# Extremes of a pair of chunks by a difference on GpSimd and fused passes on VectorE, in the FFN of an attention block

## The chip, the core and the metric

The kernel runs on one core of a Trainium2 chip. The metric is device time in microseconds (us). A core has five engines with queues of their own: TensorE (PE; PEld is its weight load), VectorE (DVE), ScalarE (ACT), GpSimd (POOL) and SyncE (SP, which only issues transfers here). An engine works through its own instructions in order; between engines, semaphores carry the order.

## What is computed

A cross-attention with a residual, and then a feed-forward network (FFN) whose two layers multiply quantized numbers, for 32 batches of 100 rows of 256:

```python
def _affine_quantize(x):
    amin, amax = (jnp.min(x), jnp.max(x))
    scale = jnp.maximum((amax - amin) / 255.0, 1e-08)
    zp = jnp.clip(jnp.round(-amin / scale) + QMIN, QMIN, QMAX)
    q = jnp.clip(jnp.round(x / scale) + zp, QMIN, QMAX)
    return (q, scale, zp)
...
    h = _qlinear(x, W1, b1)
    h = jax.nn.gelu(h, approximate=False)
    out = _qlinear(h, W2, b2)
...
x = x + _L0_xattn_ref(_layernorm(x, axis=-1), ctx_1024, ctx_1024, ...)
x = x + _L0_ffn_ref(_layernorm(x, axis=-1), L0_ffn_W1, L0_ffn_b1, L0_ffn_W2, L0_ffn_b2)
```

What matters here is `amin` and `amax` of `h`, the whole tensor after the gelu: 1024 features for 3200 rows. Nothing of the second layer can be quantized before both are known.

## The kernel before

The attention takes most of the kernel. Its last part, the residual of the last batch, ends near 1246 us of the profile; then comes the FFN.

**First layer.** `h` lies in SBUF as 128 partitions x 8 chunks of features (`fc`) x 3200 rows, in fp32. The rows are taken in five units `u`: two of 400 rows (g 0 and 1) and three of 800 (two groups of 400 each). For every unit and every chunk TensorE makes a product in PSUM (L823), and ScalarE applies the gelu on the way to `h` (L831). Below, (u, fc) names one such chunk. Between these, ScalarE rounds the input rows of later groups (`round_rows`, L738), GpSimd clips them (`bound_rows`, L752, writing `xq`), TensorE turns them (L777) and ScalarE copies them back (`turn`, L780).

**Extremes.** As soon as a span of chunks is done, VectorE takes its maximum (L838, a column of `hmax`) and its minimum (L840, a column of `hmin`), each a pass of its own over all elements of the span. `spans` says how many chunks go together: two in units 2 and 3 (1600 elements a partition), four in unit 4 (3200). `follow` and the variable `after` write out the order of VectorE's work by hand. In the end L861 and L862 reduce the columns to `ext2`, the maximum and the negated minimum of each partition.

**Parameters.** `affine_params` lets GpSimd reduce `ext2` over the partitions (`partition_all_reduce`, L108, result `alh`), and VectorE works out scale, reciprocal and bounds in a chain of tiny instructions (L110 to L126). Ahead of it, GpSimd runs an all-reduce on a dummy `g2` (L855 to L857), after its last `xq`.

**Second layer.** For ten blocks of rows ScalarE and VectorE scale `h` to integers (`ih`, L895 and L891), VectorE clips them (`hq`, L900), TensorE multiplies (`pf`, L908), VectorE adds the residual (L876), and SyncE stores. The first block is one of 128 rows. In front of it TensorE runs 18 products on an idle tile (`warm`, L151 to L156), released by a tiny product that reads the last column of `hmax`.

The tiles of the first layer lie in a pool `f1`, which is closed before the second layer's pool `f2` opens.

Of the kernel before, what the change touches and what calls it, by code (L numbers as in the profile page):

```python
# [8 lines left out]
F32 = mybir.dt.float32  # L9
BF16 = mybir.dt.bfloat16  # L10
I16 = mybir.dt.int16
AF = mybir.ActivationFunctionType
ALU = mybir.AluOpType
AX = mybir.AxisListType
# [7 lines left out]
BIG = 3.4e38  # L22
# [5 lines left out]
def kernel(  # L28
# [15 lines left out]
    nc = tc.nc  # L44
    P = 128
    B, T, D = x.shape
# [11 lines left out]
    NG = B // G  # L58
    GT = G * T
# [7 lines left out]
    const = ctx.enter_context(tc.tile_pool(name="const", bufs=1))  # L67
# [27 lines left out]
    def follow(a, b):  # L95

        tc.add_manual_dep(a.ins, b.ins.name, ORDER)
# [53 lines left out]
    def warm(ps, n, gate=None):  # L151

        if gate is not None:
            nc.tensor.matmul(ps[: gate.shape[1], : gate.shape[1]], gate, gate, start=True, stop=True)
        for _ in range(n):
            nc.tensor.matmul(ps, idle[:, :P], idle, start=True, stop=True)  # L156


    with ExitStack() as att:
# [120 lines left out]
        def v_part(b, h, s):  # L280

            c = cbuf[b % NCB]
            if s == 0:
                vs[b, h] = p1.tile([SC, NSC, E // 2], F32, tag=f"v{h}", name=f"v{b}_{h}")
            pv = bank(f"pv{b}_{h}_{s}")
            for dc in range(NDC):
                nc.tensor.matmul(  # L287
                    pv[:SC, :],
                    c[:, dc, s * SC : (s + 1) * SC],
                    wvt[h][:, dc, :],  # L290
                    start=(dc == 0),
                    stop=(dc == NDC - 1),
                )
            return nc.vector.tensor_copy(vs[b, h][:, s, :], pv[:SC, :])  # L294
# [321 lines left out]
        for i, (b, first, n) in enumerate(steps):  # L616
            g, j = b // G, b % G
# [5 lines left out]
            if b >= 1:  # L623
                for h in begun:
                    for c in range(NSC):
                        done = v_part(b, h, c)
# [9 lines left out]
            for h in ended:  # L636
                k = 2 * j + h
# [26 lines left out]
        i = len(steps) - 1  # L664
# [17 lines left out]
    f1 = ff1.enter_context(tc.tile_pool(name="f1", bufs=2))  # L682
    ps_h = ctx.enter_context(tc.tile_pool(name="ps_h", bufs=3, space=PSUM))
# [4 lines left out]
    h = hpool.tile([P, NFC, N], F32, tag="h", name="h")  # L688
# [41 lines left out]
    ixs, xqs = {}, {}  # L730

    def round_rows(g, engine, after):
        ixs[g] = f1.tile([T, G * D], I16, tag="ix", name=f"ix{g}", bufs=3)
        src = xg[g].rearrange("t b d -> t (b d)")
        if engine is nc.vector:
            done = nc.vector.tensor_scalar(ixs[g], src, rx[:T], None, ALU.mult)
        else:
            done = nc.scalar.activation(ixs[g], src, AF.Copy, bias=0.0, scale=rx[:T])  # L738
        if after is not None:
            follow(done, after)  # L740
        return done

    def bring_back(g):

        if g < len(places):
            first, n = places[g]
            nc.sync.dma_start(out=xf[g][:, :n, :], in_=rows(xb2, first, n))

    def bound_rows(g, engine, after=None):
        xqs[g] = f1.tile([T, G * D], BF16, tag="xq", name=f"xq{g}", bufs=4)  # L750

        done = engine.tensor_scalar(  # L752
            xqs[g], ixs[g], hix[:T], QMIN - QMAX, ALU.min, ALU.max
        )
        if after is not None:
            follow(done, after)
        bring_back(g)
        return done
# [5 lines left out]
    units = [(0, 1), (1, 1)] + [(g, 2) for g in range(2, NG, 2)]  # L764
# [3 lines left out]
    def turn(g, part, parts):  # L768

        if part == 0:  # L770
            xqTs[g] = f1.tile([P, NDC, GT], BF16, tag="xqT", name=f"xqT{g}", bufs=4)
        n = G // parts
        pt = ps_t.tile([P, NDC, 512], BF16, tag="pt", name=f"pty{g}_{part}")
        for dc in range(NDC):
            for j in range(n):
                k = (part * n + j) * D + dc * P
                nc.tensor.transpose(  # L777
                    pt[:, dc, j * T : (j + 1) * T], xqs[g][:, k : k + P], identb[:T, :T]
                )
        done = nc.scalar.copy(  # L780
            xqTs[g][:, :, part * n * T : (part + 1) * n * T], pt[:, :, : n * T]
        )
        if gelu is not None:
            follow(done, gelu)

    NR = 20
    hmax = f1.tile([P, NR], F32, tag="hmax", name="hmax", bufs=1)
    hmin = f1.tile([P, NR], F32, tag="hmin", name="hmin", bufs=1)
    k = 0
# [4 lines left out]
    after = scaled  # L794
    for part in range(2):
        sl = slice(part * G * D // 2, (part + 1) * G * D // 2)
        nc.scalar.activation(i0[part], src[:, sl], AF.Copy, bias=0.0, scale=rx[:T])
        after, before = nc.vector.tensor_scalar(
            xq0[:, sl], i0[part], QMIN - QMAX, hix[:T], ALU.max, ALU.min
        ), after  # L800
# [3 lines left out]
    after = round_rows(1, nc.vector, after)  # L804
    after = bound_rows(1, nc.vector, after)
# [2 lines left out]
    turned = {(0, 4): 1, (1, 2): 2, (1, 6): 3, (2, 4): 4, (2, 6): 5, (3, 4): 6, (3, 6): 7}  # L808
    for u, (g, n) in enumerate(units):
        ts = slice(g * GT, (g + n) * GT)  # L810
        spans = ((1, 1, 2, 2, 2), (2, 2, 4), (2,) * 4, (2,) * 4, (4, 4))[u]
        ends = [sum(spans[: i + 1]) for i in range(len(spans))]
        for fc in range(NFC):
            if (u, fc) in turned:
                turn(turned[u, fc], 0, 1)

            cut = 2 if (u, fc) == (0, 0) else 1
            m = GT // cut
            for part in range(cut):
                ph = ps_h.tile([P, 2, 512], F32, tag="ph", name=f"ph{u}_{fc}_{part}")  # L820
                for i in range(n):
                    for dc in range(NDC):
                        nc.tensor.matmul(  # L823
                            ph[:, i, :m],
                            w1qt[:, dc, fc * P : (fc + 1) * P],
                            xqTs[g + i][:, dc, part * m : (part + 1) * m],
                            start=(dc == 0),
                            stop=(dc == NDC - 1),
                        )
                at = slice(g * GT + part * m, g * GT + part * m + n * m)  # L830
                gelu = nc.scalar.activation(  # L831
                    h[:, fc, at].rearrange("p (k t) -> p k t", k=n),
                    ph[:, :n, :m],
                    AF.Gelu, bias=b1t[:, fc : fc + 1], scale=c1,
                )
                if fc + 1 in ends:
                    src = h[:, fc + 1 - spans[ends.index(fc + 1)] : fc + 1, at if cut > 1 else ts]
                    done = nc.vector.tensor_reduce(hmax[:, k : k + 1], src, AX.XY, ALU.max)  # L838
                    follow(done, after)
                    after = nc.vector.tensor_reduce(hmin[:, k : k + 1], src, AX.XY, ALU.min)  # L840
                    k += 1
            if (u, fc) == (0, 1):
                after = round_rows(2, nc.vector, after)

                done = bound_rows(2, nc.gpsimd, reduced)
                added = keep(B - 1, nc.gpsimd, nc.gpsimd)
                follow(added, done)
                normalize(B - 1, added, nc.gpsimd)
            if (u, fc) in rounded:
                i = rounded[u, fc]  # L850
                round_rows(i, nc.scalar, gelu)
                bound_rows(i, nc.gpsimd)

    g2 = small.tile([P, 1], F32, tag="g2", name="g2")
    nc.gpsimd.tensor_copy(g2, epst)  # L855
    nc.gpsimd.tensor_copy(g2[:T], xqs[NG - 1][:, 0:1])
    nc.gpsimd.partition_all_reduce(g2, g2, P, bass_isa.ReduceOp.max)  # L857

    ext2 = const.tile([P, 2], F32, tag="ext2", name="ext2")
    with tc.high_priority():  # L860
        nc.vector.tensor_reduce(ext2[:, 0:1], hmax[:, :k], AX.X, ALU.max)  # L861
        nc.vector.tensor_reduce(ext2[:, 1:2], hmin[:, :k], AX.X, ALU.min, negate=True)  # L862
        rh, hih, c2, _, _, found, bounds, product = affine_params(ext2, "h", scales["2"][1])
    warm(ps_h.tile([P, 512], F32, tag="ph", name="warm3"), 18, hmax[:, k - 1 : k])

    ff1.close()
    f2 = ctx.enter_context(tc.tile_pool(name="f2", bufs=2))
# [1 line left out]
    after = found  # L869
# [12 lines left out]
    for i, (first, n) in enumerate(blocks):  # L882
        hq = f2.tile([P, NFC, G * P], BF16, tag="hq", name=f"hq{i}", bufs=3)
        ts = slice(first * P, (first + n) * P)
        ih = []
        for k in range(2):
# [3 lines left out]
            if k == 1 and i in halved:  # L890
                done = nc.vector.tensor_scalar(t, h[:, sl, ts], rh, None, ALU.mult)  # L891
                follow(done, after)
                after = done
            else:
                nc.scalar.activation(t, h[:, sl, ts], AF.Copy, bias=0.0, scale=rh)  # L895
        if i == 0:
            after = bounds(after)
        for k in range(2):
            sl = slice(k * NF2, (k + 1) * NF2)
            done = nc.vector.tensor_scalar(  # L900
                hq[:, sl, : n * P], ih[k], QMIN - QMAX, hih, ALU.max, ALU.min
            )
            follow(done, after)
            after = done
# [10 lines left out]
        if i == 0:  # L915
            after = product(after)
        if i >= 2:
            done = finish(i - 2)
            follow(done, after)
            after = done  # L920
# [43 lines left out]
```

## Time and profile before

| | us |
|---|---|
| median of three runs (1339.32 to 1339.75) | 1339.72 |
| the profiled execution | 1340.4 |
| its span | 1338.6 |
| TensorE busy in the span | 1306.3 (98%) |
| VectorE busy | 779.1 (58%) |
| ScalarE busy | 696.2 (52%) |
| GpSimd busy | 96.4 (7%) |
| first gelu begins, last gelu ends | 1251.5, 1293.3 |
| first product of the second layer begins | 1312.1 |

The span is what the hardware profiler recorded from first to last instruction of one execution; the execution is 1.8 us longer. The page cuts the span into 40 slices of 33.5 us and gives each engine's busy share of a slice in tenths; the last two slices hold the FFN:

```profile
PE   9999999999999999999999999999999999999748
DVE  4666446664366554664366653664566543576897
PEclk9999999999999999999999999999999999999989
```

PEclk is the clock that TensorE was granted, in tenths of its full speed. In the groups of instructions a row reads: line, engine, operation, what is written <- what is read, shapes, count, then busy us and mean ns of one, then idle time before it and whose event ended that. In a timeline a row begins with start and duration in us, and a row of several instructions is merged; durations overlap the next start by a little, so the time that an instruction takes of its engine is read from start to start.

### The profile page before, as it was taken

To read this page: it belongs to the slowest core of one execution; us is meant where nothing else is said; L and a number is where in the kernel's file an instruction comes from. 1 tells how busy PE (TensorE), PEld (TensorE's weight loads), DVE (VectorE), ACT (ScalarE), POOL (GpSimd) and SP (SyncE) were. 2 spreads that over 40 slices of the span, in tenths; PEclk is the share of its full clock that TensorE was granted. 3 is DMA by queue.
4 is the path that set the end of the run, shared out by engine and by line. 5 is a ranking of instruction groups with operands and counts; after the bars stand their busy time and mean duration, and the time that the engine had idled before them with its cause. 6 is when DMAs were issued, how large, how long until landed. Compare 5 with 4: busy or idle time off the path is not lost.

```text
span 1338.6 us, 25468 instructions
## 1 busy us (share of the span) xinstructions
PE 1306.3 (98%) x10062; PEld 807.5 (60%) x10064; DVE 779.1 (58%) x2391; ACT 696.2 (52%) x1927; POOL 96.4 (7%) x190
## 2 busy tenths in 40 slices
PE   9999999999999999999999999999999999999748
PEld 4666556666566566666566666665666665666426
DVE  4666446664366554664366653664566543576897
ACT  2555345565355455563355454553455543554865
POOL 1000000200011000110011000110001000110200
PEclk9999999999999999999999999999999999999989
DMA  8010001000000000000000000000000000000212
GB/s 254 20 44 13 12 12 44 19 18 1 12 19 18 12 12 1 19 19 12 12 18 19 12 2 12 18 18 12 12 13 18 18 2 12 11 10 5 61 41 99
DMA packets 24864, 33.02 MB, mean 25 GB/s; under 512 B 1828, under 2 KB 22792, under 8 KB 24744
## 3 DMA queue, kind: packets, MB, share of 16 engines
q1 hardware_dynamic: 21776, 24.81, 6.3%
q0 software_dynamic: 2144, 5.38, 1.3%
q8 instruction: 79, 1.29, 0.4%
q10 hardware_dynamic: 824, 1.19, 0.3%
q14 instruction: 41, 0.34, 0.1%
HBM read 24.82 MB, written 6.55 MB: 23 GB/s over the span
## 4 chain that ended last, share of the span: by engine, by line
PE 94%; issue 3%; ACT 2%; DVE 0%; POOL 0%; POOLq 0%; DVEq 0%
PE pv L287 25%; PE pk L256 23%; PE sc L423 13%; PE av L468 10%; PE pt L373 7%; PE pq L348 6%; PE py L505 6%; PE pf L908 2%; ACT h L831 1%; PE po L489 1%; PE po L519 0%; PE ptx L336 0%; ACT ix L738 0%; ACT xqT L780 0%; PE pk L270 0%
## 5 line engine op out<-in xcount | busy, mean ns | idle before, releaser
L287 PE MATMUL pv<-wvt,c 128*128 128x512 f32 x768 | 338.3, 596 | 0.0
L256 PE MATMUL pk<-c,wkt 128*128 128x361 f32 x1016 | 314.2, 467 | 0.0
L263 ACT COPY kT<-pk 128x361 f32<-128x361 f32 x254 | 117.0, 461 | 366.4 <-PE pk L256 366.4
L404 ACT ACTIVATE p<-p,m 114x361 f32<-114x361 f32 x512 | 297.3, 590 | 7.8 <-DVE m L434 7.8
L256 PEld LDWEIGHTS pk<-c,wkt 128*128 128x128 f32 x1016 | 191.9, 190 | 113.2 <-issue 1.0
L434 DVE CUSTOM_DVE_ANT_0 p<-sc,maskt 114x361 f32<-114x361 f32 x512 | 252.2, 533 | 11.9 <-PE sc L423 6.9
L287 PEld LDWEIGHTS pv<-wvt,c 128*128 128x128 f32 x768 | 143.3, 190 | 172.1 <-issue 161.7
L385 DVE COPY pT<-pt 128x300 f32<-128x300 f32 x50 | 22.3, 468 | 351.6 <-PE pt L373 351.6
L423 PE MATMUL sc<-kT,q 64*114 64x361 f32 x1024 | 208.4, 490 | 0.0
L385 ACT COPY pT<-pt 128x300 f32<-128x300 f32 x462 | 168.9, 414 | 73.8 <-PE pt L373 71.2
L373 PEld LDWEIGHTS pt<-ident,p 50*128 50x128 f32 x3072 | 131.1, 139 | 78.0 <-issue 51.5
L449 DVE TENSOR_SCALAR p<-p,r 114x361 f32<-114x361 f32 x512 | 173.5, 402 | 2.6
L294 DVE COPY v<-pv 128x512 f32<-128x512 f32 x192 | 129.3, 679 | 28.7 <-PE pv L287 28.3
L468 PEld LDWEIGHTS av<-pT,v 128*64 128x64 f32 x3072 | 132.8, 137 | 18.5 <-ACT pT L385 15.0
L468 PE MATMUL av<-pT,v 128*64 128x100 f32 x3072 | 140.0, 250 | 0.0
L373 PE MATMUL pt<-ident,p 50*128 50x50 f32 x3072 | 133.5, 221 | 0.3 <-DVE p L449 0.3
L404 ACT ACTIVATION_READ_ACCUMULATOR p<-p,m 114x1 f32 x512 | 99.1, 194 | 0.0
L135 POOL TENSOR_TENSOR xb<-x,b2a 100x256 f32<-100x256 f32 x32 | 23.5, 733 | 900.4 <-DVE rmax L529 891.2
L348 PE MATMUL pq<-xnT,wqt 128*128 128x400 f32 x256 | 87.9, 500 | 0.2 <-ACT xnT L339 0.2
L423 PEld LDWEIGHTS sc<-kT,q 64*114 64x114 f32 x1024 | 76.7, 184 | 4.3 <-issue 0.6
L505 PE MATMUL py<-aT,wot 128*128 128x400 f32 x224 | 76.4, 499 | 0.0
L443 DVE RECIPROCAL r<-rsum 114x4 f32<-114x4 f32 (+1 forms) x131 | 22.8, 174 | 90.2 <-ACT p L404 89.9
(125 smaller groups left out, 720.0 us busy)
## 6 DMA issues: line engine op xcount, KB each, us to landing
c<-in_ctxT_dram SPq DMA_DIRECT2D x31, 361.0 KB, 3.2
x<-in_x_dram SPq DMA_DIRECT2D x8, 400.0 KB
xb<-xb POOLq DMA_DIRECT2D x32, 100.0 KB, 2.1
x<-xb SPq DMA_DIRECT2D x5, 384.0 KB, 3.1
out_dram<-ot SPq DMA_DIRECT2D x3, 384.0 KB, 2.6
wqt<-in_wq_dram SPq DMA_DIRECT2D x4, 256.0 KB
wot<-in_wo_dram SPq DMA_DIRECT2D x1, 1024.0 KB, 8.5
w<-in_w1T_dram POOLq DMA_DIRECT2D x1, 1024.0 KB, 5.5
```

What stands on the lines that cost most here:

```text
L256: nc.tensor.matmul(pk[:, :S], wkt[q][:, dc, col * P : (col + 1) * P], c[:, dc, :S], start=(dc == 0), stop=(dc == NDC - 1),)
L287: nc.tensor.matmul(pv[:SC, :], c[:, dc, s * SC : (s + 1) * SC], wvt[h][:, dc, :], start=(dc == 0), stop=(dc == NDC - 1),)
L294: return nc.vector.tensor_copy(vs[b, h][:, s, :], pv[:SC, :])
L348: nc.tensor.matmul(pq[:, :GT], wqt[q][:, dc, pair * P : (pair + 1) * P], xnTs[g][:, dc, :], start=(dc == 0), stop=(dc == NDC - 1),)
L373: nc.tensor.transpose(pts[k][:SC, (h * NSC + c) * TH : (h * NSC + c + 1) * TH], pb[ks, h0 + h, c * SC : (c + 1) * SC], ident[ks, ks],)
L385: copies.append(copy(pT[:, :, k, :], src))
L404: done = nc.scalar.activation(s, s, AF.Exp, bias=ms[h], scale=-1.0, accum_out=rsum[:, h : h + 1])
L423: nc.tensor.matmul(pss[h][:TP, :S], qbuf[pair // PAIRS][k * DK : (k + 1) * DK, pair % PAIRS, j, :, :].rearrange("p k t -> p (k t)")[:, :TP ...
L434: found = nc.vector.tensor_tensor_reduce(pb[:, h, :S], pss[h][:TP, :S], maskt, 1.0, BIG, ALU.add, ALU.min, ms[h])
L449: nc.vector.tensor_scalar(s, s, r[:, h : h + 1], None, ALU.mult)
L468: nc.tensor.matmul(av[k * DK : (k + 1) * DK, (pair - p0) * T : (pair - p0 + 1) * T], vs[b, pair // HP][:, c, h * DK : (h + 1) * DK], pTs[i ...
L505: nc.tensor.matmul(py[:, :GT], wot[:, c, dc * P : (dc + 1) * P], aT[:, c, :, :].rearrange("p j t -> p (j t)"), start=(c == 0), stop=(c == ...
```

## The change

Four pairs of neighbouring chunks, (2,6) with (2,7), (3,6) with (3,7), (4,0) with (4,1) and (4,6) with (4,7), are taken out of the reductions. With a the first and b the second of a pair, GpSimd forms r = max(a - b, 0) in two instructions. Then max(a, b) = r + b, and -min(a, b) = r - a. VectorE runs one fused pass for each of the two: it adds or subtracts two tensors of 800 elements a partition, and takes the maximum of the results and of a starting column. The elementwise result goes to `other`, which nobody reads. Unit 4 is reduced in pairs now, and its chunks 2 to 5 still by two passes each.

The starting columns chain the passes: pair (2,6) begins from -BIG and runs in the middle of unit 3; after the last reduction, `hmax` and `hmin` are reduced, merged with its result, and handed through pairs (3,6), (4,0) and (4,6); the last writes `ext2`. The dummy all-reduce now follows the last difference, and the idle products wait for the first column of pair (4,0).

```diff
+    paired = {(2, 6): (3, 3), (3, 6): (3, 7), (4, 0): (4, 1), (4, 6): (4, 7)}
+    diffs = {}
+
+    def difference(u, fc):
+        g, n = units[u]
+        ts = slice(g * GT, (g + n) * GT)
+        a, b = h[:, fc, ts], h[:, fc + 1, ts]
+        r = f1.tile([P, 2 * GT], F32, tag="r", name=f"r{u}_{fc}", bufs=4)
+        nc.gpsimd.tensor_tensor(r, a, b, ALU.subtract)
+        nc.gpsimd.tensor_scalar(r, r, 0.0, None, ALU.max)
+        diffs[u, fc] = r, a, b
+
+    def pair(u, fc, ext, behind, after):
+
+        r, a, b = diffs[u, fc]
+        for col, (x, op) in enumerate(((b, ALU.add), (a, ALU.subtract))):
+            other = f1.tile([P, 2 * GT], BF16, tag="other", name=f"other{u}_{fc}_{col}", bufs=1)
+            done = nc.vector.tensor_tensor_reduce(
+                other, r, x, 1.0, ext[col], op, ALU.max, behind[:, col : col + 1]
+            )
+            follow(done, after)
+            after = done
+        return after
...
-        spans = ((1, 1, 2, 2, 2), (2, 2, 4), (2,) * 4, (2,) * 4, (4, 4))[u]
+        spans = ((1, 1, 2, 2, 2), (2, 2, 4))[u] if u < 2 else (2,) * 4
...
-                if fc + 1 in ends:
+                if fc + 1 in ends and (u, fc - 1) not in paired:
...
+            for p, at in paired.items():
+                if at == (u, fc):
+                    difference(*p)
+            if (u, fc) == (3, 3):
+                after = pair(2, 6, (-BIG, -BIG), exts[0], after)
...
-    nc.gpsimd.tensor_copy(g2[:T], xqs[NG - 1][:, 0:1])
+    nc.gpsimd.tensor_copy(g2, diffs[4, 6][0][:, 0:1])
...
+    done = nc.vector.tensor_reduce(exts[1][:, 0:1], hmax[:, :k], AX.X, ALU.max)
+    follow(done, after)
+    after = nc.vector.tensor_reduce(exts[1][:, 1:2], hmin[:, :k], AX.X, ALU.min, negate=True)
+    done = nc.vector.tensor_tensor(exts[1], exts[1], exts[0], ALU.max)
+    follow(done, after)
+    after = done
+    cols = [exts[1][:, 0:1], exts[1][:, 1:2]]
+    for p, behind in (((3, 6), exts[2]), ((4, 0), exts[3]), ((4, 6), ext2)):
+        after = pair(*p, cols, behind, after)
+        cols = [behind[:, 0:1], behind[:, 1:2]]
     with tc.high_priority():
-        nc.vector.tensor_reduce(ext2[:, 0:1], hmax[:, :k], AX.X, ALU.max)
-        nc.vector.tensor_reduce(ext2[:, 1:2], hmin[:, :k], AX.X, ALU.min, negate=True)
         rh, hih, c2, _, _, found, bounds, product = affine_params(ext2, "h", scales["2"][1])
-    warm(ps_h.tile([P, 512], F32, tag="ph", name="warm3"), 18, hmax[:, k - 1 : k])
+    warm(ps_h.tile([P, 512], F32, tag="ph", name="warm3"), 18, exts[3][:, 0:1])
```

In the order in which the scheduler puts GpSimd's instructions, difference (2,6) stands between the `xq` of groups 5 and 6, and the other three stand behind the last `xq`, ahead of the dummy all-reduce. On VectorE pair (2,6) stands behind the reductions of (3,2) and (3,3). The instructions of the other engines keep their order.

## The prediction

> **What bounds the kernel now.** I read the page first (span 1338.6 us; the profiled execution took 1340.4 us, so 1.8 us lie around the span), then the waits from 1225 us on, then each engine's timeline there. For 1240 us TensorE is the limit, and the change touches nothing of that. It touches the last stretch: the first layer of the FFN, 1250 to 1309 us, whose extremes must be known before anything of the second layer can start. Two rows of the waits (who waited, for whom, total us, times, longest):
>
> ```profile
> POOL alh L108 <- DVE ext L862: 20.6, 1, 20.6
> ACT ih L895 <- DVE rsh L112: 17.3, 1, 17.3
> ```
>
> GpSimd and ScalarE are idle there, waiting for VectorE. VectorE's timeline (start, duration, instruction, in brackets the idle time before):
>
> ```profile
> 1264.41 1.82 DVE L838 TENSOR_REDUCE hmax<-h 128x1 f32<-128x1600 f32 x1 [0.65 <-ACT h L831]
> ...
> 1283.41 1.81 DVE L840 TENSOR_REDUCE hmin<-h 128x1 f32<-128x1600 f32 x1
> 1285.14 1.81 DVE L838 TENSOR_REDUCE hmax<-h 128x1 f32<-128x1600 f32 x1
> ...
> 1305.67 3.48 DVE L840 TENSOR_REDUCE hmin<-h 128x1 f32<-128x3200 f32 x1
> 1309.07 0.16 DVE L861 TENSOR_REDUCE ext<-hmax 128x1 f32<-128x19 f32 x1
> 1309.86 0.16 DVE L110 TENSOR_TENSOR sch<-alh 128x1 f32<-128x1 f32 x1 [0.50 <-POOL alh L108]
> ```
>
> Since 1264.41 us no row has a gap: VectorE reduces without pause until 1309.2 us. From start to start a pass over 1600 elements takes 1.73 us (1283.41 to 1285.14), over 3200 it takes 3.39. The data are there much earlier; ScalarE's and GpSimd's timelines:
>
> ```profile
> 1283.81 9.45 ACT L831 ACTIVATE h<-ph,b1t,cx 128x800 f32<-128x800 f32 x10
> ...
> 1310.52 19.71 ACT L895 ACTIVATE ih<-h,rsh 128x512 int16<-128x512 f32 x15 [17.26 <-DVE rsh L112]
> ```
> ```profile
> 1278.13 1.12 POOL L752 TENSOR_SCALAR xq<-ix,hix 100x1024 bf16<-100x1024 int16 x1 [6.83 <-ACT ix L738]
> ...
> 1282.17 0.19 POOL L856 CAST g<-xq 100x1 f32<-100x1 bf16 x1
> 1288.46 0.38 POOL L857 PARTITION_ALL_REDUCE g<-g  x1 [6.11 <-issue]
> 1309.46 0.37 POOL L108 PARTITION_ALL_REDUCE alh<-ext  x1 [20.62 <-DVE ext L862]
> ```
>
> The last gelu ends at 1293.26, 16 us before the last reduction. So in this stretch a microsecond of VectorE is a microsecond of the kernel, as long as nothing else becomes later than it. One candidate is in the last fence: in front of g's all-reduce GpSimd stands still for 6.1 us, with no event to explain it; alh's all-reduce, which follows one, starts at once. g is there to pay that pause early. From the end of the work before it (1282.10) to the end of that all-reduce (1288.84) are 6.74 us; today hidden under 20 us of waiting.
>
> **The change, part by part.**
>
> 1. Removed from VectorE: the two passes over pair (2,6) and pair (3,6), 4 x 1.73 = 6.91; unit 4's four passes over 3200, 4 x 3.39 = 13.57; the two closing reductions, 0.28. Sum 20.76 us.
>
> 2. Added to VectorE: unit 4's chunks 2 to 5 in four passes over 1600, 6.91; closing steps of three dependent tiny instructions, some 0.2 each by the spacing of L110 to L112 (1309.86, 1310.06, 1310.24), 0.6; and eight fused passes over 800 elements. The same operation is in the trace with one operand in PSUM:
>
> ```profile
> 1232.49 0.42 DVE L529 CUSTOM_DVE_ANT_0 x<-x,po 100x256 f32<-100x256 f32 x1 [2.76 <-PE po L489]
> 1232.84 0.08 DVE L529 DVE_READ_ACCUMULATOR2_ANT rmax<- 100x1 f32 x1
> 1232.96 0.43 DVE L533 BATCH_NORM_STATS2 st<-x 100x6 f32<-100x256 f32 x1
> ```
>
> The follower that needs its result starts 0.47 us later. In the new code each second pass waits for the first (both write `other`, one buffer), so I take this dependent spacing and 1.042 ns an element (the slope between 1600 and 3200 elements of the reductions rounds to it): 0.47 + 544 x 1.042 ns = 1.04 us. Bounds: without the dependence L434's 361 elements repeat every 0.455 us, which gives 0.91; two SBUF operands at two cycles each would give 1.87. The tiny rows exclude the latter: L710, two SBUF operands of 32, takes 192 ns, L712 with one 188. Eight passes: 8.3 us (7.3 to 9). Sum added 15.8, so VectorE ends **4.95 us** earlier, at about 1304.4 instead of 1309.35.
>
> 3. Added to GpSimd: four times a subtraction and a maximum over 128x800 fp32, in front of that pause. Nearest rows (mean ns, then idle before):
>
> ```profile
> L135 POOL TENSOR_TENSOR xb<-x,b2a 100x256 f32<-100x256 f32 x32 | 23.5, 733 | 900.4 <-DVE rmax L529 891.2 <-issue 9.0
> L752 POOL TENSOR_SCALAR xq<-ix,hix 100x1024 bf16<-100x1024 int16 x6 | 6.7, 1112 | 24.4 <-ACT ix L738 17.3 <-DVE ix L736 7.1
> L142 POOL TENSOR_SCALAR x<-x,mv,rstd 100x256 f32<-100x256 f32 x1 | 1.2, 1243 | 0.1
> ```
>
> A 100x1 copy or add costs 0.18 to 0.25 there, so L135 pays some 2.1 ns an element and the subtraction takes 1.9 us. For the maximum the rows disagree: L752 (minimum and maximum, 16 bit) pays 0.85 ns, hence 0.92 us; L142 (fp32 and in place, as here, but subtract and multiply by two columns) pays 3.9 ns, hence 3.4 us. The Trainium skill (GPSIMD Engine Reference, Performance versus the Vector engine) puts bodies of up to two operations at 1.03 cycles an element, an estimate of 0.69 us plus start, and lists a chain of dependent fp32 adds and multiplies at 4 cycles. That fits both rows: the operation decides, and a maximum belongs with L752. I take 2.9 us for a pair of instructions plus the small wait between them, 2.95; ends 2.8 and 5.3.
>
> When: order on GpSimd is two xq, difference (2,6), two xq, the other three, then g. Gelu (2,7) ends about 1275.2 (second of four that begin at 1273.08, 0.91 us apart), so difference (2,6) runs to 1278.2 and xq's 1278.13 is touched by 0.1 us, which vanishes before ScalarE's 1280.58 copy needs it. Difference (3,6) runs from about 1286.05 to 1289, (4,0) to 1292, (4,6) from 1293.3 to 1296.3. Then 6.74 us: g is done at **1303.0**, 1.4 us ahead of VectorE. The 20 us of cover shrink to that: this is the step that is late next.
>
> 4. The fused passes beside GpSimd. VectorE reaches pair (2,6) at 1285.14 and leaves it at 1287.2; difference (3,6) becomes ready at 1286.05. The Trainium skill (SBUF — State Buffer, Who interferes with whom) says a VectorE instruction with two SBUF inputs and a GpSimd instruction that reads SBUF exclude each other for a whole instruction, the later blocking. The trace has no such overlap: its fused passes read one operand from PSUM, and reductions of 800 beside L752 at 1255.65 took their usual 0.97. By the row the cost is 0. By the rule it is either 0 for VectorE (GpSimd waits 1.1 us and has it back before 1293), or, should GpSimd slip between the two passes, one subtraction, 1.9 us, all on the path. I take 0 and keep 1.9. The three last pairs (1298.2 to 1304.4) come after the last difference.
>
> 5. The warm-up. Its gate moves from the last hmax to the first pass of pair (4,0), about 1301.3. Before, 6.3 us passed from gate (1305.8) to second layer (1312.11), and TensorE ran into it with no gap; the granted clock was 0.50 in the windows from 1295 to 1310 and 1.00 from 1311. Now VectorE still needs 3.1 us after the gate, and 2.55 as before from all-reduce to first matmul: 5.65, so the warm-up would be 0.65 late. Block 0 ended 0.27 before block 1 was ready, so **0.35 us** are lost. From block 1 on TensorE streams (192 matmuls, 21.1 us) as before.
>
> Sum: 1340.4 - 4.95 + 0.35 = 1335.8 for the profiled execution; it was 0.7 above the median shown (1339.72), so the forecast is **1335.1 us**.
>
> **The rivals.**
>
> - A, the sum above: 1335.1, own range 1334.0 to 1336.3 (fused passes 0.91 to 1.1, clock 0.3 either way). Chance 0.52.
> - B, the lock costs VectorE one subtraction at pair (2,6): saving 2.75, 1337.0. For it: the two are ready within 0.2 us of each other. Against: no row shows it. Chance 0.20.
> - C, slower: GpSimd becomes the bound. At L142's rate a difference takes 5.3 us. Difference (2,6) then ends at 1280.55, xq is 2.4 us late, gelu 1.65 late; the other differences run back to back from 1287.65 to 1303.55; g is done at 1310.3 and the all-reduce starts 0.9 us later than before. Worse, the warm-up has by then ended some 5 us before the second layer; the clock fell about 2.2 us after TensorE's last matmul at 1291.4 and took 4.7 us of work to return, so 4.7 us of matmuls run at half speed, 2.3 us lost. Together 1342.9. It decides from about 4.5 us a difference (all-reduce later than 1307.3, gain 2.2, clock loss 2.3). For it: L142 shares type and placement. Against: the operation. Chance 0.20.
> - D, the passes over two SBUF operands run at half rate: eight times 0.83 more, 1341.4. L710 speaks against it. Chance 0.08.
>
> **How the numbers follow.** A measurement of this kernel tells 0.2% (2.7 us) from no change, so faster means below 1337.0. A is faster; B lies on the edge and is halved; C falls half on milder values that end within the bound (a difference of 4.5 us) and half on slower; D ends inside or outside about evenly. Faster 0.62, same 0.24, slower 0.14. The range takes A, B and the milder part of C: 1333.9 to 1340.5.
>
> **What would show it.** Right: fused rows of about 1.0 us, L861's successors at 1297.6, ext2 complete near 1304.4, GpSimd's all-reduce of g before it, subtraction 1.9 and maximum 0.9, no gap between the passes of pair (2,6). Wrong: a maximum of 2 us or more, VectorE waiting for r, a gap inside pair (2,6), or a granted clock of 0.5 after the second layer has begun.

## The result, and the profile after

The changed kernel takes 1337.53 us (median of 17 runs, 1336.64 to 1338.92), the one before 1340.05 (17 runs, 1339.26 to 1340.74): a ratio of 0.9983 (95% interval 0.9976 to 0.9990). It is faster, by 2.5 us where 4.6 were forecast; that lies inside the 0.2% which the prediction called no change, and its forecast of faster by more than that did not come true.

The profiled execution has a span of 1335.1 us, 3.5 less, but its first layer also began 0.85 us earlier, for reasons in front of the change. So I measure inside the stretch, from the first gapless reduction on. VectorE's timeline of the changed kernel (start, duration, instruction, idle time before):

```profile
1263.56 1.82 DVE L867 TENSOR_REDUCE hmax<-h 128x1 f32<-128x1600 f32 x1 [0.63 <-ACT h L860]
...
1285.30 0.99 DVE L806 CUSTOM_DVE_ANT_0 other<-r,h 128x800 bf16<-128x800 f32 x1
1286.22 0.08 DVE L806 DVE_READ_ACCUMULATOR2_ANT ext<- 128x1 f32 x1
1286.22 1.81 DVE L867 TENSOR_REDUCE hmax<-h 128x1 f32<-128x1600 f32 x1
...
1296.90 0.45 DVE L897 TENSOR_TENSOR ext<-ext,ext 128x2 f32<-128x2 f32 x1
1297.50 1.05 DVE L806 CUSTOM_DVE_ANT_0 other<-r,h,ext 128x800 bf16<-128x800 f32 x1
...
1304.20 0.08 DVE L806 DVE_READ_ACCUMULATOR2_ANT ext<- 128x1 f32 x1
1306.30 0.16 DVE L110 TENSOR_TENSOR sch<-alh 128x1 f32<-128x1 f32 x1 [2.01 <-POOL alh L108]
```

The last line carries the result. VectorE is done at 1304.28, after 40.72 us of work that took 44.94 before: 4.2 us saved. Then it stands idle for 2.0 us, where it was 0.5. What it waits for is on GpSimd's timeline:

```profile
1285.93 2.14 POOL L797 TENSOR_TENSOR r<-h 128x800 f32<-128x800 f32 x1 [4.42 <-ACT h L860]
1288.17 2.20 POOL L798 TENSOR_SCALAR r<-r 128x800 f32<-128x800 f32 x1
1290.34 1.93 POOL L797 TENSOR_TENSOR r<-h 128x800 f32<-128x800 f32 x1
1292.36 2.21 POOL L798 TENSOR_SCALAR r<-r 128x800 f32<-128x800 f32 x1
1294.53 1.88 POOL L797 TENSOR_TENSOR r<-h 128x800 f32<-128x800 f32 x1
1296.49 2.20 POOL L798 TENSOR_SCALAR r<-r 128x800 f32<-128x800 f32 x1
1298.76 0.93 POOL L891 COPY g<-r 128x1 f32<-128x1 f32 x1
1305.53 0.38 POOL L892 PARTITION_ALL_REDUCE g<-g  x1 [5.83 <-issue]
1305.82 0.44 POOL L108 PARTITION_ALL_REDUCE alh<-ext  x1
```

The maximum (L798) takes 2.2 us, not 0.9. The three last differences run back to back, the last does not even start when its gelu is done but 1.4 us later, and the pause in front of g's all-reduce comes behind all of it. `alh` follows g without a gap: GpSimd, not VectorE, is now last. One thing more stands here: the copy of a single column (L891) takes 0.93 us, where such a copy (L856) took 0.19 before. It begins while a fused pass (1298.60) is running.

TensorE, finally, did not hold the second layer up. It stood idle for 1.29 us until the first `hq` came:

```profile
1301.53 5.73 PE L156 MATMUL warm<-idle 128*128 128x512 bf16 x17 [0.33 <-issue]
1308.55 1.03 PE L950 MATMUL pf<-w2qt,hq 128*128 128x256 bf16 x8 [1.29 <-DVE hq L942]
1309.85 21.14 PE L950 MATMUL pf<-w2qt,hq 128*128 128x256 bf16 x192 [0.27 <-DVE hq L942]
```

The account, from the first gapless reduction to block 1 of the second layer: 48.99 us before, 46.29 now. VectorE's work is 4.22 less, the wait in front of L110 1.51 more, the rest unchanged (3.54 and 3.55). Together 2.7 less, beside 2.5 in the medians.

### The profile page after: what moved, and what is told of

It is laid out like the page before. It is cut to its first block, busy times and chain, and to the rows that moved or that the text cites. A ratio compares the mean times of both kernels' runs of the same rounds, so it can differ in the third digit from the quotient of the medians.

```text
span 1335.1 us, 25493 instructions
## 1 busy us (share of the span) xinstructions
PE 1306.2 (98%) x10062; PEld 807.5 (60%) x10064; DVE 774.2 (58%) x2404; ACT 695.8 (52%) x1927; POOL 113.6 (9%) x198
## 3 DMA queue, kind: packets, MB, share of 16 engines
q8 instruction: 79, 1.29, 0.4%
## 4 chain that ended last, share of the span: by engine, by line
PE 94%; POOL 2%; issue 2%; ACT 1%; DVE 1%; POOLq 0%; DVEq 0%
PE pv L287 25%; PE pk L256 23%; PE sc L423 13%; PE av L468 10%; PE pt L373 7%; PE pq L348 6%; PE py L505 6%; PE pf L950 2%; PE po L489 1%; ACT h L860 1%; POOL r L797 1%; POOL r L798 1%; PE po L519 0%; PE ptx L336 0%; PE ph L852 0%
```

## The experiments

The theory to test: GpSimd's chain (differences, pause, all-reduce) sets the end, because its maximum costs 2.2 us. The rivals: VectorE's own work still sets it; or the two engines hold each other up when both read SBUF, and the copy of 0.93 us is a sign of that.

**The change again** (e0_after), as the measure for the rest.

> The changed kernel again, as the measure for the others on the same chip: 2.5 us below the kernel before, VectorE idle for 2.0 us in front of L110.

It took 1337.52 us (21 runs), ratio 0.9983 (0.9976 to 0.9989); the wait in front of L110 was 2.3 us.

**One pair fewer** (e2_three_pairs).

```diff
-    paired = {(2, 6): (3, 3), (3, 6): (3, 7), (4, 0): (4, 1), (4, 6): (4, 7)}
+    paired = {(2, 6): (3, 3), (3, 6): (3, 7), (4, 0): (4, 1)}
...
-    for p, behind in (((3, 6), exts[2]), ((4, 0), exts[3]), ((4, 6), ext2)):
+    for p, behind in (((3, 6), exts[2]), ((4, 0), ext2)):
```

The dummy follows (4, 0) and the warm-up's gate reads `exts[1]`.

> The changed kernel with three pairs: (4,6) goes back to two reductions over 1600. GpSimd theory (its chain of differences, pause and all-reduce sets the end): GpSimd is done with g near 1301, 4 us earlier; VectorE works 1.1 us longer, ext2 near 1305.4, and the wait in front of L110 falls to 0.5; the time is 0.2 to 0.6 us below the changed kernel although VectorE does more. VectorE theory (its work alone sets the end): 1.1 us above the changed kernel.

1336.48 us, ratio 0.9975 (0.9966 to 0.9984): 1.0 below the changed kernel by the medians, where 0.2 to 0.6 were expected; the intervals overlap a little. VectorE does more and the kernel is not slower. The wait in front of L110 is 0.51 again, and `alh` waits 3.26 us for VectorE. The VectorE theory, which asked for 1.1 us more, falls.

**The last maximum on ScalarE** (e4_relu_act).

```diff
-        nc.gpsimd.tensor_scalar(r, r, 0.0, None, ALU.max)
+        if (u, fc) != (4, 6):
+            nc.gpsimd.tensor_scalar(r, r, 0.0, None, ALU.max)
...
     nc.gpsimd.partition_all_reduce(g2, g2, P, bass_isa.ReduceOp.max)
+    r = diffs[4, 6][0]
+    nc.scalar.activation(r, r, AF.Relu)
```

> The changed kernel with the maximum of pair (4,6) on ScalarE (relu), which is idle after the last gelu[...]. GpSimd theory: 2.2 us leave GpSimd's chain, g is done near 1303.5, the wait in front of L110 falls from 2.0 to 0.5, and the time is 1.5 us below the changed kernel (4 below the kernel before). Lock theory (the fused passes hold GpSimd up, or the reverse, wherever it stands): the copy in front of g stays near 0.9 us or a pass is delayed, gain under 0.8. VectorE theory: no change.

1335.58 us, ratio 0.9967 (0.9954 to 0.9979), 1.9 below the changed kernel. Its GpSimd timeline:

```profile
1297.05 0.19 POOL L892 COPY g<-r 128x1 f32<-128x1 f32 x1
1303.22 0.47 POOL L893 PARTITION_ALL_REDUCE g<-g  x1 [5.98 <-issue]
1304.65 0.37 POOL L108 PARTITION_ALL_REDUCE alh<-ext  x1 [0.96 <-DVE ext L807]
```

With 2.2 us out of the chain, `alh` waits for VectorE again, and the copy, which now comes in front of VectorE's last pairs, is back at 0.19. VectorE gained a little, too: the instruction that merges the columns (L897 of the changed kernel, two tensors of two elements) takes 0.16 us here, where no GpSimd work runs beside it, and took 0.45 in the changed kernel, inside GpSimd's last maximum:

```profile
1297.48 0.16 DVE L900 TENSOR_TENSOR ext<-ext,ext 128x2 f32<-128x2 f32 x1
```

The GpSimd theory stands: taking its work away gains, taking VectorE's work back does not lose.

**Why the maximum takes 2.2 us** (p1_probe, p2_forms). Single instructions after the kernel's last result.

> The kernel before, with single GpSimd instructions over 128x800 appended after its last result (its own output is unchanged, its time is not compared). First GpSimd alone, VectorE idle. If the operation alone decides, fp32 maximum costs 2.2 us in place and out of place alike and a multiplication the same or more; if being in place decides, the out-of-place maximum falls to 0.9; if fp32 data decide, only the maximum over int16 costs 0.9 and the fp32 multiply, the copy and the bf16 output cost some 2 us too. Then tiny copies, a subtraction and a maximum beside twelve fused VectorE passes, and again beside twelve reductions. If the two engines exclude each other for whole instructions, the tiny copy (0.19 us alone) takes up to 1 us beside the fused passes and the subtraction (1.9 alone) comes out longer or opens gaps of 1.9 us between VectorE's passes; beside reductions nothing changes. If not, both halves look alike.

GpSimd alone in p1_probe, in this order: subtraction; maximum in place; maximum out of place; the same to bf16; maximum then minimum; multiplication; maximum then minimum from int16; copy:

```profile
1345.68 1.86 POOL L940 TENSOR_TENSOR r<-h 128x800 f32<-128x800 f32 x1 [6.88 <-issue]
1347.63 2.25 POOL L941 TENSOR_SCALAR r<-r 128x800 f32<-128x800 f32 x1
1349.97 2.20 POOL L942 TENSOR_SCALAR r<-r 128x800 f32<-128x800 f32 x1
1352.14 2.20 POOL L943 TENSOR_SCALAR rb<-r 128x800 bf16<-128x800 f32 x1
1354.42 2.89 POOL L944 TENSOR_SCALAR r<-r 128x800 f32<-128x800 f32 x1
1357.39 2.23 POOL L945 TENSOR_SCALAR r<-r 128x800 f32<-128x800 f32 x1
1359.70 2.88 POOL L946 TENSOR_SCALAR rb<-ri 128x800 bf16<-128x800 int16 x1
1362.65 0.85 POOL L947 COPY r<-r 128x800 f32<-128x800 f32 x1
```

Neither place nor type matters: one operation costs 2.2, two cost 2.9, only a copy runs at 0.85. But then xq's clipping, two operations over 1024 elements in 1.1 us, is the odd one. What sets it apart was the question of p2_forms.

> The kernel before, with single GpSimd instructions appended after its last result (VectorE idle; its own output is unchanged, its time is not compared): what made the clipping of xq (0.85 ns an element) so much cheaper than the maximum (2.5). If the column operand decides, minimum with a column and maximum with a constant over 128x800 fp32 costs 0.9 us; if the 16-bit types decide only together with the column, only the int16 rows with a column cost 0.9; if the 100 partitions decide, the 100x1024 rows cost 1.1 whatever their operands, and 128x1024 fp32 2.8.

Its rows: maximum with a column (L945); minimum with a column, then maximum with a constant, from fp32 (L946) and int16 (L948); minimum, then maximum, both constants (L951); subtract and multiply by columns (L949); maximum over 100 and over 128 partitions (L952, L953):

```profile
1353.70 2.27 POOL L945 TENSOR_SCALAR r<-r,col 128x800 f32<-128x800 f32 x1
1355.95 0.92 POOL L948 TENSOR_SCALAR rb<-ri,col 128x800 bf16<-128x800 int16 x1
1356.86 0.92 POOL L946 TENSOR_SCALAR r<-r,col 128x800 f32<-128x800 f32 x1
1357.86 1.04 POOL L951 TENSOR_SCALAR wb<-wi 100x1024 bf16<-100x1024 int16 x1
1358.99 3.06 POOL L949 TENSOR_SCALAR r<-r,col 128x800 f32<-128x800 f32 x1
1362.02 2.77 POOL L952 TENSOR_SCALAR wg<-wf 100x1024 f32<-100x1024 f32 x1
1364.88 2.77 POOL L953 TENSOR_SCALAR wg<-wf 128x1024 f32<-128x1024 f32 x1
```

None of my three guesses (column, type, partitions) was right. Minimum and then maximum, in that order, costs 0.92 with a column (L946), and without one 1.04 over 1024 elements (L951); maximum then minimum cost 2.9 in p1_probe; a maximum alone is slow with either operand. What is quick is one pair of operations in one order. Why it is quick is not shown, and a minimum alone was not tried.

**The quick form in the kernel** (e6_form).

```diff
-        nc.gpsimd.tensor_scalar(r, r, 0.0, None, ALU.max)
+        nc.gpsimd.tensor_scalar(r, r, bigt, 0.0, ALU.min, ALU.max)
```

`bigt` is a column of 3.4e38, so the minimum changes nothing.

> The changed kernel with its maximum written as xq's clipping is: minimum with a column that holds 3.4e38, then maximum with 0. If the column operand makes it cheap, it costs 0.9 instead of 2.2, g is done near 1303.5 and the time is 1.5 to 2 us below the changed kernel. If not, two operations cost 2.9, each difference takes 0.65 longer, g is some 2 us later and so is the kernel: 1339.5. Either answer follows the GpSimd chain at a slope of one.

The maximum takes 0.93 us, g is done at 1302.6, `alh` waits 1.85 us for VectorE; 1335.49 us, ratio 0.9971 (0.9963 to 0.9979), 2.0 below the changed kernel. Only this one term of the sum is altered, and the kernel gains from it until VectorE is last.

One thing is open. Nine of the 14 runs took 1334.8 to 1335.6 us, the other five 1337.3 to 1339.3, and the profile is of one of the nine. In it the subtraction of (3,6) begins 0.2 us behind the second pass of pair (2,6) (1285.83 and 1285.65). Had it come ahead of that pass, the pass would have waited (case B of the prediction), which would fit the 2 us between the groups; no trace shows it.

**VectorE again** (e5_columns): with e4_relu_act's relu, the fused passes no longer hang on each other.

```diff
-        for col, (x, op) in enumerate(((b, ALU.add), (a, ALU.subtract))):
-            other = f1.tile([P, 2 * GT], BF16, tag="other", name=f"other{u}_{fc}_{col}", bufs=1)
...
+        done = nc.vector.tensor_tensor_reduce(
+            other, r, b, 1.0, -BIG, ALU.add, ALU.max, hmax[:, k : k + 1]
+        )
...
+        after = nc.vector.tensor_tensor_reduce(
+            spare, r, a, 1.0, -BIG, ALU.subtract, ALU.max, hmin[:, k : k + 1]
+        )
```

`hmin` holds negated minima, and the warm-up's gate moves one pair earlier.

> The kernel with the relu of the last pair on ScalarE, and now VectorE's fused passes all start from -3.4e38 into columns of their own, with two scratch tiles, so that no pass waits for the one before; the warm-up is released one pair earlier. Passes then follow each other after 0.91 us instead of 1.1, ext2 is complete about 2 us earlier than in e4_relu_act. VectorE theory (without GpSimd's delay VectorE sets the end again, microsecond for microsecond): 2 us below e4_relu_act. GpSimd theory (g, done about 1 us ahead of ext2 there, is now the later one): about 1 us below it, and 0.3 from the warm-up: 1334.3.

1334.11 us, ratio 0.9955 (0.9942 to 0.9967), 1.5 below e4_relu_act: as the GpSimd theory said. Passes follow each other after 0.91 us, ext2 is complete at 1303.1, and L110 still waits 1.04 us, because g is done only at 1303.7.

**Both together** (e7_clip_columns): e5_columns with all maxima on GpSimd, now `tensor_scalar(r, r, BIG, 0.0, ALU.min, ALU.max)`.

> e5_columns with the maxima of all four pairs back on GpSimd, written as minimum with 3.4e38 and then maximum with 0, both constants, no column. If the pair of operations in that order is what GpSimd does quickly (p2_forms), each takes 0.93 us as with a column; g is done near 1303.0 by e5_columns's clock (0.7 earlier), ext2 near 1302.9, and the time is 0.3 to 0.6 us below e5_columns: 1333.6. If the column matters after all, 2.9 us a maximum and some 1338.

1333.55 us, ratio 0.9951 (0.9938 to 0.9963): the quickest of all, 6.5 us below the kernel before and 4 below the change. Against e5_columns the intervals don't separate the two; the profiles show the step, a wait in front of L110 of 0.50 us where it was 1.04:

```profile
1294.84 0.85 POOL L798 TENSOR_SCALAR r<-r 128x800 f32<-128x800 f32 x1
1295.76 0.19 POOL L894 COPY g<-r 128x1 f32<-128x1 f32 x1
1301.78 0.52 POOL L895 PARTITION_ALL_REDUCE g<-g  x1 [5.83 <-issue]
1302.38 0.37 POOL L108 PARTITION_ALL_REDUCE alh<-ext  x1
```

ext2 is complete at 1302.27, g at 1302.3: the two engines end together.

**The shared memory access.** The second half of p1_probe ran the same GpSimd instructions beside twelve fused passes and beside twelve reductions. GpSimd's column copy, subtraction and maximum, first beside fused passes, then beside reductions:

```profile
1365.67 0.97 POOL L970 COPY col<-h 128x1 f32<-128x1 f32 x1
1366.60 2.63 POOL L971 TENSOR_TENSOR r<-h 128x800 f32<-128x800 f32 x1
1369.32 2.83 POOL L972 TENSOR_SCALAR r<-r 128x800 f32<-128x800 f32 x1
...
1378.57 0.18 POOL L970 COPY col<-h 128x1 f32<-128x1 f32 x1
1378.71 1.88 POOL L971 TENSOR_TENSOR r<-h 128x800 f32<-128x800 f32 x1
1380.67 2.20 POOL L972 TENSOR_SCALAR r<-r 128x800 f32<-128x800 f32 x1
```

Beside reductions all three are as alone; beside fused passes each is longer by part of a pass. VectorE's passes at that moment:

```profile
1366.52 0.98 DVE L955 CUSTOM_DVE_ANT_0 o<-r,h 128x800 bf16<-128x800 f32 x1
...
1367.44 2.65 DVE L955 CUSTOM_DVE_ANT_0 o<-r,h 128x800 bf16<-128x800 f32 x1
...
1370.02 1.62 DVE L955 CUSTOM_DVE_ANT_0 o<-r,h 128x800 bf16<-128x800 f32 x1
```

The pass that meets the subtraction takes 1.67 us more, the one that meets the maximum 0.64 more. So the contention that the prediction took from the Trainium skill (SBUF — State Buffer, Who interferes with whom) is real here. The page states it for a VectorE instruction with two SBUF inputs and a GpSimd instruction that reads SBUF. That the first comer holds the access for its whole instruction it states of VectorE's two-port modes, and the prediction carried that over. For the subtraction it nearly holds (1.67 of 1.9 us); for the maximum, 2.2 us long, it does not: that held VectorE up for only 0.64. The changed kernel agrees. Its pass at 1297.50 began 1.0 us into the maximum at 1296.49, and neither was longer than alone (1.05 and 2.20 us), while L897, 0.4 us into the same maximum, was held up for 0.3. L897 is a plain maximum of two tensors, so the hold-up is not peculiar to the fused operation.

**What it costs where it strikes** (e8_five_pairs): e7_clip_columns with another choice of pairs.

```diff
-    paired = {(2, 6): (3, 3), (3, 6): (3, 7), (4, 0): (4, 1), (4, 6): (4, 7)}
+    paired = {(2, 4): (2, 5), (2, 6): (3, 3), (3, 6): (3, 7), (4, 0): (4, 1), (4, 2): (4, 3)}
```

The passes of (2,4) stand behind unit 2, those of (2,6) behind (3,5), and those of (3,6) in front of (4,5)'s reduction; the warm-up's gate moves along.

> The same with five pairs, (2,4), (2,6), (3,6), (4,0) and (4,2); (4,6), the last to be known, goes back to VectorE. VectorE's work falls by 1.6 us, and g can start 1.5 us earlier. Without collisions: 0.8 below e7_clip_columns. Lock theory: fused passes of (2,6) and (3,6) now stand beside GpSimd's subtractions, and a pass that finds one running waits up to 1.7 us; one such wait takes the gain away (0 to 1 us above e7_clip_columns), shown by a fused pass of over 1.2 us.

1339.50 us, ratio 0.9995 (0.9987 to 1.0004): 6 us worse than e7_clip_columns, no better than the kernel before. I had expected at most one collision; every one of the first six fused passes met one:

```profile
1275.37 2.71 DVE L806 CUSTOM_DVE_ANT_0 other<-r,h 128x800 bf16<-128x800 f32 x1 [0.99 <-POOL r L798]
...
1278.01 1.62 DVE L810 CUSTOM_DVE_ANT_0 spare<-r,h 128x800 bf16<-128x800 f32 x1
...
1289.92 2.20 DVE L806 CUSTOM_DVE_ANT_0 other<-r,h 128x800 bf16<-128x800 f32 x1
...
1293.61 2.64 DVE L806 CUSTOM_DVE_ANT_0 other<-r,h 128x800 bf16<-128x800 f32 x1
```

Over the six passes the excess above 0.98 us is 6.5 us; VectorE also idled 1 us for the first r. Less the 1.6 us of work saved, that makes 5.9, beside 6.0 measured. The pass at 1278.01 met a quick maximum, and that held it up for 0.64 us, as the slow one had in p1_probe.

## Why the prediction was right or wrong

**Parts 1 and 2, VectorE's work: nearly.** Forecast 4.95 us less, measured 4.22. The passes of pair (2,6) took 0.97 each from start to start, better than 1.04; those that start from a column took 1.06 to 1.24 with their waits (six in 6.8 us, 0.5 more than forecast), and the three closing steps 0.9 instead of 0.6. The 0.3 between are L897's, which Part 4 has to answer for. The bound of two cycles an element never came near.

**Part 3, GpSimd's work: wrong in one term, and this decides the result.** The term is the maximum, put at 0.92 us and measured at 2.2. The subtraction was right (1.9). I saw the two rows that disagree, L752 and L142, and chose L752 because a maximum is the same kind of operation; the rule of the Trainium skill (GPSIMD Engine Reference, Performance versus the Vector engine: up to two operations at 1.03 cycles an element) seemed to settle it. p1_probe and p2_forms show that this price holds for a copy and for minimum-then-maximum, and not for a maximum alone, nor for maximum-then-minimum. L752 was the exception. L142, subtract and multiply, was nearer to the general case: two operations took 2.9 to 3.06 us over 800 elements, one took 2.2. (The 4 cycles that the prediction set beside L142 stand in another section of the same page, Performance pitfalls for Q7 kernels.) A maximum of 2 us or more was the prediction's own first sign of being wrong. The estimated end of g, 1303.0 by the clock of the profile before, became 1306.8 by the same clock: 2.5 us from the three last differences, some 0.7 from gelus that came later by that clock (0.4 of it they already had ahead of the first difference; for the rest, an xq behind that difference was late for ScalarE's copy), 0.5 from g's copy and pause. The margin of 1.4 us was gone, and the kernel lost 1.5 us of its gain in front of L110.

**Part 4, the collision: right that no fused pass is held up, by timing, but not that VectorE pays nothing.** Where VectorE's pair (2,6) met GpSimd's subtraction (3,6), GpSimd came second and waited 0.2 us; g's copy, behind a pass of pair (3,6), waited 0.74. The prediction looked at the fused passes alone; L897 also reads two tensors in SBUF, met the last maximum, and cost VectorE 0.3 us, which its wait for g covered. Case B, a pass held up for a subtraction, did not happen in the profiled execution, but its price was nearly right: 1.67 us in p1_probe, against 1.9.

**Part 5, the warm-up: not reached in the changed kernel.** TensorE had been ready for 1.3 us when the first block came, since the late g covered the difference. Where VectorE was last again, it did show: in e4_relu_act and e6_form the first product followed the idle products without a gap, 2.7 and 2.6 us behind L110, where 2.25 were enough before. That is 0.4 to 0.5 us late; 0.65 were forecast.

**The cases.** A's saving was there, but not on the path; what happened is the milder part of C: GpSimd became the bound at 4.2 to 4.4 us a difference, below the 4.5 at which I let it turn the sign. The range held the time because it was drawn to take that part of C in; the likeliest value was 2.4 us too low. That the time lies within 0.6 us of case B's 1337.0 is coincidence, since B's mechanism is not in the profile.

## What to carry to other kernels

When a bound engine is relieved by an idle one, write down the idle one's new chain to its end, what used to be hidden under its idleness included, and give each term the price of the general case, unless a row of the very same operation says otherwise; here one term, too low by 1.3 us and paid in three differences back to back, made up the better part of the 3.7 us by which g came late, and that took 1.5 of the 4.2 us saved on VectorE. A fused pass that reads two tensors from SBUF collides with a neighbour's instructions beside which a plain reduction ran undisturbed, so such passes belong where the neighbour is quiet. And when the new bound is known, look for its cheap form before moving work back: one more operation in the same instruction gained 2 us.

## What the runs showed of the hardware

- GpSimd over 128x800 fp32: copy 0.85 us, minimum then maximum 0.85 to 0.93, subtraction of two tensors 1.9, a single maximum or multiplication 2.2, maximum then minimum 2.9, subtract and multiply by columns 3.06. In the forms tried, data type, destination in place, a column for a constant, and 100 partitions for 128 changed this by less than 0.1 us.
- In front of g's all-reduce, behind GpSimd's other work, GpSimd stood still for 5.8 to 6.2 us with no event to explain it; `alh`'s all-reduce, which follows g's, needed no such pause.
- A VectorE instruction over two tensors in SBUF and a GpSimd instruction that reads SBUF held each other up: a copy of one column took 0.97 us instead of 0.19, a fused pass 2.65 instead of 0.98 beside a subtraction and 1.62 beside a maximum. A pass that began 1.0 us into a maximum was not held up. Reductions beside the same instructions took no longer.
- A fused pass over 800 elements that starts from a column took 1.05 us, from a constant 0.98; with the waits for a predecessor, the step from pass to pass was 1.0 to 1.2 and without them 0.91.
